# Cross-attention and FFN on one core: probabilities turned in 32x32 blocks by VectorE in the middle groups, and weighted sums in sixteen tiles of the array

## The chip, the cores and the metric

The kernel runs on one core of one Trainium2 chip. The metric is the time of one execution in microseconds of the device. Before the change three runs gave 793.26, 792.1 and 794.7 us, with a median of 793.26 us. All arithmetic on the path spoken of here is float32.

## The reference, cut to what matters

There are 16 batches of 128 rows and 1024 columns, with 32 query heads of 32 columns; four query heads share one of 8 key and value heads.

```
Q = layernorm(x) @ Wq + bq;  K = ctx @ Wk + bk;  V = ctx @ Wv + bv
w = softmax(Q K^T / sqrt(32))            # per batch and head, 128 x 128
x = x + (w @ V) @ Wo + bo
x = x + scale * (ei(layernorm(x)) @ kernel)   # ei: last 20% of the columns times -4
```

What the change concerns is `w @ V`: for each batch and head, probabilities of 128 queries by 128 keys times values of 128 keys by 32 columns. TensorE contracts over partitions, so the keys must lie on the partitions of both operands; the exponentials leave ScalarE with the queries on the partitions.

## The kernel before, in words

The 16 batches go in eight groups of two (`GB = 2`). A group has four **attention steps**, one for each batch `b` and half `a` of the heads (16 query heads each): the steps `q = 0..3` of line 970 have b0 a0, b1 a0, b0 a1, b1 a1. Beside these steps TensorE has **dense work**: the output projection of the group before (`out_proj`, matmuls on line 661), keys and values of the next group (`prep_k`, `prep_v`, line 322), queries of the next group (`prep_q`, line 450) and the FFN (`ffn`, line 322).

The order of all instructions is written by a planner in the kernel, the class `Stream`. Dense work is a queue of generators; each piece yields its estimated length, which advances a planned clock. `later(us, fn)` puts a small piece of other work (a normalization, a division, a transpose) at a planned time; `run(until)` emits pieces and what has come due. The planned lengths set the order in which instructions stand on each engine and nothing else: the engines then wait for one another only through data.

One attention step is `attend` (line 754) and `weighted` (line 605). `scores` (line 560) issues 16 matmuls of 32 contraction rows, four for each of four PSUM tiles (`ps_sc`, four buffers of one bank); a tile `i` holds four heads (`NG = 4`) that share a key head. For each tile VectorE finds the negated maximum (line 579), ScalarE does four exponentials with their row sums (line 583), VectorE takes the reciprocal (line 594) and multiplies (line 595). Then `turn` has TensorE transpose the four 128x128 blocks (line 600) into PSUM and ScalarE copies the result to SBUF (line 602). At the step's end `weighted` does four matmuls of 128 keys by 32 columns, with 512 moving columns each (line 610), into one PSUM bank, the four in four column strips of the array, and ScalarE copies the bank (line 618). The next step's scores follow at once.

On TensorE each float32 matmul that is not a transpose stands in the program as two pairs of a weight load and a matmul with the same operands (5024 pairs on the page); these are called **passes** here. A transpose is one pass.

The first group (group 0) and the last (group 7) have loops of their own; groups 1 to 6 are the **middle groups**, 24 attention steps. All loads and stores go through SP's queue in the planned order; the weights of the projections come as pieces of 512 KB into a ring of eight buffers (`fetch`, line 219). The normalized rows of the FFN of early groups go through DRAM (`through_dram`, line 301), and VectorE then turns and splits them (`split_blocks`, line 719), at the planned delays `FBACK` (line 822).

## Time and profile before

| | |
|---|---|
| median of three runs | 793.26 us |
| the profiled execution: its own time / its span | 793.75 / 792.0 us |
| granted TensorE clock, mean | 0.997 |
| busy: TensorE / VectorE / ScalarE | 770.7 / 484.9 / 322.7 us |
| DMA | 190.31 MB, mean 240 GB/s |
| one matmul record of line 610 (512 columns) | 619 ns mean, 256 records |
| one matmul record of line 567 (128 columns) | 283 ns mean, 1024 records |
| VectorE, one 32x32-block transpose of 128x512 float32 (lines 348, 370, 727) | 699 to 703 ns |
| VectorE, the multiplication on line 595 | 716 ns mean, 128 of them |
| ScalarE, copy of 128x512 from PSUM (lines 602, 618) | 591 and 585 ns |
| ScalarE, activation of 128x128 (lines 583, 437) | 369 and 368 ns |

Records of matmuls overlap, since the array is pipelined: a mean length is not what one of them costs. What it costs is the distance to the next one's start, which the chain of waits and the timeline give. The rows of one engine in the timeline are merged where they follow one another; "idle before" stands in brackets with what ended it.

### The profile page before, as it was taken

What the parts mean: (1) busy time and instruction counts of PE and PEld (TensorE: products, weight loads), DVE (VectorE), ACT (ScalarE), POOL (GpSimd) and SP (SyncE); (2) the same over time, 40 slices, a digit from 0 to 9 for tenths busy, and PEclk for the clock granted to TensorE, in tenths of its full rate; (3) what the DMA queues carried; (4) which work ended last, traced back from release to release, by engine and by line L of the source; (5) the groups of instructions that cost most, each with busy time, mean ns of one, the idle gap of its engine ahead of it and who ended that gap; (6) DMA issues with size and microseconds to landing.
All of it is one profiled execution on the core that took longest, in us unless ns stands there. A gap on an engine that the chain in (4) does not pass through costs nothing.

```text
span 792.0 us, 13741 instructions
## 1 busy us (share of the span) xinstructions
PE 770.7 (97%) x5024; PEld 572.8 (72%) x5024; DVE 484.9 (61%) x882; ACT 322.7 (41%) x1261; POOL 107.3 (14%) x133
## 2 busy tenths in 40 slices
PE   5998999999999999999999999999999999999997
PEld 4886794589746996479855898568974799546566
DVE  1258647756766667466774667755676756667442
ACT  0254764434344443344533444343434445466100
POOL 1153703020010102020020200102001100100300
PEclk9999999999999999999999999999999999999999
DMA  9999799979698776978688786977769567562502
GB/s 211 361 299 296 251 382 390 267 209 305 221 310 232 239 239 214 314 210 264 219 264 263 196 287 212 302 233 209 260 217 321 190 204 243 184 195 81 205 34 80
DMA packets 98483, 190.31 MB, mean 240 GB/s; under 512 B 8016, under 2 KB 57168, under 8 KB 98416
## 3 DMA queue, kind: packets, MB, share of 16 engines
q1 hardware_dynamic: 96544, 187.73, 73.5%
q10 hardware_dynamic: 1728, 1.57, 1.0%
q8 instruction: 40, 0.66, 0.3%
q14 instruction: 27, 0.22, 0.1%
q0 software_dynamic: 144, 0.14, 0.1%
HBM read 160.04 MB, written 29.36 MB: 239 GB/s over the span
## 4 chain that ended last, share of the span: by engine, by line
PE 89%; DMA 4%; DVE 2%; issue 2%; POOL 1%; ACT 0%; SPq 0%; POOLq 0%
PE f L322 15%; PE o_u L661 13%; PE q_u L450 13%; PE o_v L661 7%; PE tpp L600 7%; PE q_v L450 6%; PE v L322 5%; PE k L322 5%; PE sc L567 4%; PE av L610 4%; PE q L322 3%; PE q_c L450 3%; PE o_c L661 3%; DMA piece<-o 1%; DMA wv_sb<-in_L_xattn_Wv_dram 1%
## 5 line engine op out<-in xcount | busy, mean ns | idle before, releaser
L583 ACT ACTIVATE p<-sc,negm 128x128 f32<-128x128 f32 x512 | 181.4, 369 | 140.0 <-DVE negm L579 75.9
L602 ACT COPY pt<-tpp 128x512 f32<-128x512 f32 x128 | 74.5, 591 | 143.8 <-PE tpp L600 143.4
L579 DVE TENSOR_REDUCE negm<-sc 128x4 f32<-128x512 f32 x128 | 86.7, 680 | 53.8 <-PE sc L567 53.7
L322 PE MATMUL f<-wf_sb,x2l 128*128 128x512 f32 x256 | 105.4, 412 | 0.0
L583 ACT ACTIVATION_READ_ACCUMULATOR p<-sc,negm 128x1 f32 x512 | 105.3, 206 | 0.0
L322 PE MATMUL f<-wf_sb,x2h 128*128 128x512 f32 x256 | 101.1, 395 | 0.0
L595 DVE TENSOR_TENSOR p<-p,inv 128x512 f32<-128x512 f32 x128 | 91.6, 716 | 4.4
L450 PE MATMUL q_u<-t,piece 128*128 128x128 f32 x672 | 80.9, 275 | 0.0
L600 PEld LDWEIGHTS tpp<-ident,p 128*128 128x128 f32 x512 | 62.0, 141 | 25.5 <-issue 17.0
L600 PE MATMUL tpp<-ident,p 128*128 128x128 f32 x512 | 75.9, 273 | 4.5 <-DVE p L595 3.1
L450 PEld LDWEIGHTS q_u<-t,piece 128*128 128x128 f32 x672 | 77.9, 192 | 0.0
L184 POOL TENSOR_TENSOR x<-x,bo_b 128x256 f32<-128x256 f32 x64 | 54.1, 871 | 154.2 <-DMA x<-in_x_dram 94.0
L322 PE MATMUL v<-wv_sb,cT 128*128 128x256 f32 x256 | 61.9, 391 | 9.4 <-DMA wv_sb<-in_L_xattn_Wv_dram 9.2
L661 PE MATMUL o_v<-piece,s 128*128 128x512 f32 x128 | 60.4, 598 | 0.5 <-DVE x L675 0.5
L322 PEld LDWEIGHTS v<-wv_sb,cT 128*128 128x128 f32 x256 | 48.3, 196 | 15.8 <-issue 9.2
L661 PE MATMUL o_u<-piece,s 128*128 128x512 f32 x128 | 59.1, 594 | 0.6 <-DVE x L675 0.6
L322 PE MATMUL k<-cT,wk_sb 128*128 128x256 f32 x256 | 58.1, 380 | 1.2 <-DVE cT L348 1.2
L661 PE MATMUL o_u<-piece,yT 128*128 128x512 f32 x128 | 58.5, 599 | 0.0
L322 PEld LDWEIGHTS f<-wf_sb,x2l 128*128 128x128 f32 x256 | 48.2, 188 | 11.0 <-issue 1.1
L322 PEld LDWEIGHTS f<-wf_sb,x2h 128*128 128x128 f32 x256 | 48.2, 188 | 10.2 <-issue 0.5
L322 PEld LDWEIGHTS k<-cT,wk_sb 128*128 128x128 f32 x256 | 47.9, 190 | 10.5 <-issue 2.6
L567 PEld LDWEIGHTS sc<-kT,qT 32*128 32x128 f32 x1024 | 31.5, 186 | 26.5 <-issue 26.5
(83 smaller groups left out, 932.5 us busy)
## 6 DMA issues: line engine op xcount, KB each, us to landing
piece<-o SPq DMA_DIRECT2D x64, 512.0 KB, 4.7
piece<-q SPq DMA_DIRECT2D x56, 512.0 KB, 5.1
piece<-in_L_xattn_Wq_dram SPq DMA_DIRECT2D x50, 512.0 KB, 5.3
piece<-in_L_xattn_Wo_dram SPq DMA_DIRECT2D x48, 512.0 KB, 4.6
xn<-in_x_dram SPq DMA_DIRECT2D x16, 512.0 KB, 6.7
x<-in_x_dram SPq DMA_DIRECT2D x16, 512.0 KB, 4.8
ctx<-in_ctx_dram SPq DMA_DIRECT2D x60, 128.0 KB, 6.6
out_dram<-x SPq DMA_DIRECT2D x15, 512.0 KB, 2.7
```

The lines of the kernel that those rows point to most:

```text
L184: lambda cut=cut: nc.gpsimd.tensor_add(x_t[:, cut], x_t[:, cut], bo_b[:, cut]) and None,
L322: nc.tensor.matmul(mm, lhsT=lhsT, rhs=rhs, start=k == 0, stop=k == n - 1)
L450: nc.tensor.matmul(mm if part is None else mm[:, part], lhsT=lhsT, rhs=rhs, start=start and n == k == 0, stop=k == len(some) - 1, skip_gro ...
L567: nc.tensor.matmul(tiles[i][:, g], lhsT=qT[rows, g], rhs=kT[rows, a, cols], start=True, stop=True,)
L579: nc.vector.tensor_reduce(negm, tile_, AX.X, ALU.max, negate=True)
L583: nc.scalar.activation(p[:, g], tile_[:, g], AF.Exp, bias=negm[:, g : g + 1], accum_out=total[:, g : g + 1],)
L595: nc.vector.tensor_mul(p, p, inv.unsqueeze(2).to_broadcast([P, NG, S]))
L600: nc.tensor.transpose(tp[:, g], p[:, g], ident)
L602: nc.scalar.copy(pt, tp)
L610: nc.tensor.matmul(mm[i * HD : (i + 1) * HD], lhsT=vs[b][:, h * HD : (h + 1) * HD], rhs=pts[i], start=True, stop=True,)
L661: nc.tensor.matmul(mm, lhsT=lhsT[:, 2 * k + c], rhs=w[:, c], start=start and k == c == 0, stop=k == c == 1, skip_group_check=True,)
```

## The change

In the middle groups alone:

- **Turning.** The TensorE transposes and the ScalarE copies of `turn` go. VectorE transposes each tile of probabilities in place, in 32x32 blocks (`turn_blocks`). Block (k, t) of a head then has key `32 t + r` on partition `32 k + r` and the queries of block k along the row.
- **Scaling.** For tiles 0 and 1 of a step VectorE makes the reciprocal only and ScalarE multiplies, in four activations with a scale by row (`scale_rows`). Tiles 2 and 3 are scaled on VectorE as before.
- **Weighted sums.** `weighted_blocks` has 64 matmuls of 32 keys by 32 columns with 128 moving columns, 16 for each `t`, one on each of the 16 tiles of 32x32 of the array; the four `t` accumulate. The result lies in four PSUM banks (a bank for each row strip `k`), from which one ScalarE copy gathers `yT`.
- **PSUM.** The pool `ps_sc` holds one tile of four banks instead of four of one; the scores and the weighted sums of the middle groups take turns in it. Scores have one tile of four banks in all groups.
- **Values.** Since each row strip needs the values of all keys on its own 32 partitions, `prep_v` stores the values of a middle batch to DRAM (128 KB), and `load_values` reads them back four times (four DMAs of 128 KB) into one half of `pt_all`, a constant tile in place of the four buffers `pt`. The first and last groups use `pt_all` for turned probabilities as `pt` was used.
- **Order.** The planned length of a middle step goes from 23.2 to 21.5 (in group 6 from 21.0 to 19.6). `weighted_blocks` stands 4.0 planned us ahead of the step's end, and dense work follows it before the next scores: 1.72 us in the steps q = 0, 1.7 to 3.3 us in the others, by the durations that the same pieces have in the trace of before. `FBACK` goes from 22 and 24 to 16 and 18, so that the rows of the FFN are turned and split sooner.

```diff
-    ps_sc = ctx.enter_context(tc.tile_pool(name="ps_sc", bufs=4, space=PSUM))
+    ps_sc = ctx.enter_context(tc.tile_pool(name="ps_sc", bufs=1, space=PSUM))
...
             vs[b] = v
+            if GB <= b < B - GB:
+                stream.later(2.0, lambda b=b, v=v: nc.sync.dma_start(out=v_dram[b], in_=v) and None)
...
-        tiles = [ps_sc.tile([P, NG, S], FP, tag="sc", name=f"sc_{b}_{a}_{i}") for i in range(NI)]
+        sc = ps_sc.tile([P, NI, NG, S], FP, tag="sc", name=f"sc_{b}_{a}")
...
+    def scale_rows(p, inv):
+        for g in range(NG):
+            nc.scalar.activation(p[:, g], p[:, g], AF.Copy, scale=inv[:, g : g + 1])
+
+    NK = S // HD
+    pt_all = const.tile([P, NI, NG * S], FP, name="pt_all")
...
+    def repeated(b):
+        vr = pt_all[:, 2 * (b % GB) : 2 * (b % GB) + 2].rearrange("p i n -> p (i n)")
+        return vr.rearrange("p (t n) -> p t n", t=NK)
+
+    def load_values(b):
+        for k in range(NK):
+            nc.sync.dma_start(
+                out=repeated(b)[k * HD : (k + 1) * HD],
+                in_=v_dram[b].rearrange("(t r) n -> r t n", t=NK),
+            )
+
+    def turn_blocks(p):
+        blocks = p.rearrange("p g (t k) -> p g t k", t=NK)
+        nc.vector.transpose(blocks, blocks)
+
+    def weighted_blocks(b, a, pts):
+        av = ps_sc.tile([P, NK, NG, S], FP, tag="sc", name=f"av_{b}_{a}")
+        for t in range(NK):
+            for i in range(NI):
+                head = slice(i * HD, (i + 1) * HD)
+                for k in range(NK):
+                    rows = slice(k * HD, (k + 1) * HD)
+                    nc.tensor.matmul(
+                        av[head, k, :, :HD],
+                        lhsT=repeated(b)[rows, t, a * P + i * HD : a * P + (i + 1) * HD],
+                        rhs=pts[i][rows, :, t * HD : (t + 1) * HD],
+                        start=t == 0,
+                        stop=t == NK - 1,
+                    )
+        yTs[b, a] = work.tile(S4, FP, tag="yT", name=f"yT{b}_{a}", bufs=4)
+        nc.scalar.copy(yTs[b, a].rearrange("p g (k q) -> p k g q", k=NK), av[:, :, :, :HD])
...
+                def by_vector():
+                    divide(b, a, i, p, total)
+                    turned()
+                def by_both():
+                    inv = inverse(b, a, i, total)
+                    stream.later(1.6, lambda: scale_rows(p, inv))
+                    stream.later(3.6, turned)
+                def turned():
+                    turn_blocks(p)
+                    pts[i] = p
...
+                if length is None:
+                    stream.later(2.3, by_both if i < 2 else by_vector)
...
-    FBACK = ((7.0, 22.0), (8.0, 24.0))
+    FBACK = ((7.0, 16.0), (8.0, 18.0))
...
-            length = 17.4 if first else 23.2 if grp < NGRP - 2 else 21.0
+            length = 17.4 if first else 21.5 if grp < NGRP - 2 else 19.6
...
+                    pts = attend(b, a)
+                    stream.run(start + length - 4.0)
+                    stream.run(stream.now, lambda: None in pts)
+                    weighted_blocks(b, a, pts)
+                    stream.now += 2.1
...
+                        stream.run(start + length)
+                if q == 2 * NA - 1 and first:
+                    load_values(nxt * GB)
+                if q >= 2 * NA - (1 if first else 2) and nxt < NGRP - 1:
+                    load_values(nxt * GB + q % GB)
```

More of the change, by code (lines that the diff above doesn't have):

```diff
@@ L567, in scores @@
                 nc.tensor.matmul(
-                    tiles[i][:, g],
-                    lhsT=qT[rows, g],
-                    rhs=kT[rows, a, cols],
-                    start=True,
-                    stop=True,
+                    sc[:, i, g], lhsT=qT[rows, g], rhs=kT[rows, a, cols], start=True, stop=True
                 )
-        return tiles
+        return sc
     def exponentials(b, a, i, tile_):
@@ L590, in exponentials, with inverse, divide @@
         return p, total
-    def divide(b, a, i, p, total):
+    def inverse(b, a, i, total):
         inv = small.tile([P, NG], FP, tag="inv", name=f"inv_{b}_{a}_{i}")
         nc.vector.reciprocal(inv, total)
+        return inv
+    def divide(b, a, i, p, total):
+        inv = inverse(b, a, i, total)
         nc.vector.tensor_mul(p, p, inv.unsqueeze(2).to_broadcast([P, NG, S]))
+    def scale_rows(p, inv):
[3 more added lines that the diff above has]
+    pt_all = const.tile([P, NI, NG * S], FP, name="pt_all")
+    v_dram = [dram.tile([P, KV], FP, name=f"v_dram{b}") for b in range(B)]
     def turn(b, a, i, p):
@@ L600, in turn @@
             nc.tensor.transpose(tp[:, g], p[:, g], ident)
-        pt = work.tile([P, NG, S], FP, tag="pt", name=f"pt_{b}_{a}_{i}", bufs=4)
-        nc.scalar.copy(pt, tp)
-        return pt
+        nc.scalar.copy(pt_all[:, i].rearrange("p (g s) -> p g s", g=NG), tp)
+        return True
     def weighted(b, a, pts):
@@ L612, in weighted @@
                 lhsT=vs[b][:, h * HD : (h + 1) * HD],
-                rhs=pts[i],
+                rhs=pt_all[:, i],
                 start=True,
@@ L618, in weighted @@
         nc.scalar.copy(yTs[b, a], mm)
+    def repeated(b):
[25 more added lines that the diff above has]
+        yTs[b, a] = work.tile(S4, FP, tag="yT", name=f"yT{b}_{a}", bufs=4)
+        nc.scalar.copy(
+            yTs[b, a].rearrange("p g (k q) -> p k g q", k=NK), av[:, :, :, :HD]
+        )
     x2Ts, x2ns, x2stats = {}, {}, {}
@@ L752, in ffn, with attend @@
             nc.sync.dma_start(out=out[b], in_=x_t)
-    def attend(b, a, length):
-        tiles = scores(b, a)
+    def attend(b, a, length=None):
+        sc = scores(b, a)
         stream.now += 1.2
@@ L762, in first, with by_tensor @@
             def first(i=i):
-                p, total = exponentials(b, a, i, tiles[i])
-                stream.later(2.3, lambda: divide(b, a, i, p, total))
-                def third():
+                p, total = exponentials(b, a, i, sc[:, i])
+                def by_vector():
+                    divide(b, a, i, p, total)
+                    turned()
+                def by_both():
+                    inv = inverse(b, a, i, total)
+                    stream.later(1.6, lambda: scale_rows(p, inv))
[3 more added lines that the diff above has]
+                    pts[i] = p
+                def by_tensor():
                     pts[i] = turn(b, a, i, p)
                     return 0.45
-                stream.later(length / 2 - 3.0, third)
+                if length is None:
+                    stream.later(2.3, by_both if i < 2 else by_vector)
+                else:
+                    stream.later(2.3, lambda: divide(b, a, i, p, total))
+                    stream.later(length / 2 - 3.0, by_tensor)
             stream.later(0.7 + 2.4 * i, first)
@@ L972 @@
                 start = stream.now
-                pts = attend(b, a, length)
-                if q == 2 * NA - 1:
-                    stream.run(start + length - 2.0, lambda: stream.queue)
-                else:
-                    stream.run(start + length - 2.0)
-                stream.run(stream.now, lambda: None in pts)
-                weighted(b, a, pts)
-                stream.now += 1.0
+                if first:
+                    pts = attend(b, a, length)
+                    if q == 2 * NA - 1:
+                        stream.run(start + length - 2.0, lambda: stream.queue)
+                    else:
+                        stream.run(start + length - 2.0)
+                    stream.run(stream.now, lambda: None in pts)
+                    weighted(b, a, pts)
+                    stream.now += 1.0
+                else:
+                    pts = attend(b, a)
+                    stream.run(start + length - 4.0)
+                    stream.run(stream.now, lambda: None in pts)
+                    weighted_blocks(b, a, pts)
+                    stream.now += 2.1
+                    if q == 2 * NA - 1:
+                        stream.run(start + length, lambda: stream.queue)
+                    else:
+                        stream.run(start + length)
[3 more added lines that the diff above has]
+                    load_values(nxt * GB + q % GB)
         stream.add(
```

## The prediction

> **What bounds the kernel now.** I read the page's first part, then the busy time by stretch for one whole middle group, then the chain of waits inside that group. The stretch from 430.96 to 524.96 us is one period: the same product of the output projection starts at both ends, and the periods before it have the same length.

> ```profile
> PE 770.7 (97%) x5024; PEld 572.8 (72%) x5024; DVE 484.9 (61%) x882; ACT 322.7 (41%) x1261; POOL 107.3 (14%) x133
> ```

> ```profile
> core 0: us, PE busy (x) PEld busy (x) DVE busy (x) ACT busy (x) POOL busy (x), PEclk, DMA share, GB/s
> ...
> 430.96:524.96 94.00, 94.00 (x634) 70.72 (x633) 61.19 (x112) 38.62 (x156) 9.10 (x12) 1.00 0.78 247
> ```

> TensorE is busy through the whole 94.00 us at full clock; VectorE has 33 us to spare and ScalarE 55. So a middle group lasts as long as TensorE's own work, and what TensorE no longer does shortens it, until another engine's result comes late. The chain, in order of time, shows what the removed work costs:

> ```profile
> 444.77 0.44 PE tpp L600 x4
> 445.21 1.73 PE v L322 x8
> 446.94 0.44 PE tpp L600 x4
> 447.37 2.59 PE v L322 x12
> 449.96 1.00 PE av L610 x8
> 450.96 1.10 PE sc L567 x32
> 452.06 3.77 PE q_u L450 x32
> ```

> Only TensorE appears. Four transposes take 0.44 us, the weighted sums of a step (8 passes) 1.00 us, the scores (32 passes) 1.10 us.

> **Removed from TensorE.** Shares of this chain over the period: transposes 7.4%, weighted sums 4.2%, together 11.6% of 94.0 = 10.9 us, or 2.73 us for each of four steps (4 x 0.435 + 0.995). In 24 steps that is 65.5 us.

> **Added to TensorE: the one large unknown.** A step gets 64 matmuls, which as float32 are 128 passes of 128 moving columns. The trace has no matmul of 32x32, so I bound it by the two tiled ones, here as the timeline of the weight loads has them.

> ```profile
> 426.88 0.16 PEld L610 LDWEIGHTS av<-pt,v 128*32 128x32 f32 x8 [0.76 <-issue]
> 426.88 1.07 PE L610 MATMUL av<-pt,v 128*32 128x512 f32 x8
> ...
> 427.87 0.98 PEld L567 LDWEIGHTS sc<-kT,qT 32*128 32x128 f32 x32 [0.84 <-issue]
> 427.87 1.17 PE L567 MATMUL sc<-kT,qT 32*128 32x128 f32 x32
> ```

> All eight weight loads of the weighted sums fall within 0.16 us, though the matmuls last 1.07. In the single records four matmuls start 7 ns apart on four strips, and the next four one pass later: 112 ns later for the scores' 128 columns, about 0.45 us for 512. Different strips thus run beside one another. The scores' 32 passes on four strips are eight waves of 112 ns = 0.90 us, and 1.10 in the chain, so entering and leaving costs 0.2.

> - Low end: all sixteen tiles run at once, as four do now. 128 / 16 = 8 waves x 112 ns = 0.9, plus 0.2 = **1.1 us**.
> - High end: no more than the four at once that the trace shows. 128 / 4 = 32 waves x 112 ns = 3.6, plus 0.2 = **3.8 us**.
> - Between them: the rate at which TensorE's sequencer hands out instructions. A dense matmul gives it 111 ns or more for a pair, so that it is never seen as a limit now, but a 16-tile burst of 256 instructions in 1.1 us would ask for 4 ns each. The nearest records are two semaphore waits of TensorE with eight loads and matmuls between them, at 49.862 and 49.987 us: the queue was empty there. The same distance of 0.125 us stands at 138.671. A wait itself takes 51 ns, which leaves 74 ns for eight instructions, 9.25 ns each or 18.5 ns a pass. At waits inside dense stretches the sequencer is 17 pairs ahead of the array, so 17 of the 128 are already queued. The other 111 x 18.5 ns = 2.05 us, and I add 0.05 for the entry that this does not cover: **2.1 us**.

> I take 2.1: it rests on records of this sequencer, and the low end needs a rate twice as high as any that the trace shows with an empty queue. Per step 2.73 - 2.1 = 0.63 us is saved, in 24 steps **15.1 us**. With the ends: 39 us saved at 1.1, 26 us lost at 3.8.

> [...]

> **VectorE.** Per period 16 block transposes are added at 0.70 us (the 128x512 float32 rows of lines 348, 370 and 727 are 699 to 703 ns), and 8 multiplications at 0.716 go: +11.2 - 5.7 = +5.5 us, so 66.7 of some 91.5 us. The reciprocals stay. This hides under TensorE as long as the last tile of a step is turned before its weighted sums come. Now the last multiplication of a middle step ends 11.5 to 12.8 us after the scores. Four transposes (+2.8), two multiplications less (-1.4), and, in the third step of a group, 2.1 us of the FFN rows' turning and splitting that `FBACK` moves ahead of it, put it at 13 to 16.5 us. The dense work between scores and sums, by the durations in the trace, is 17.2 to 18.0 us in groups 1 to 5, 14.6 to 15.4 in group 6. Covered by 1 to 4 us in the former, by nearly nothing in the latter: I add **1 us** in all, for waits in group 6. Without the cover each us late costs 24 us; the bounds are 0 and 1.5 us a step, the second if ScalarE's and VectorE's turns fall badly.

> **ScalarE.** Per period 16 copies of 591 ns go (9.5 us) and 32 scalings of 128x128 come (nearest row: 368 ns on line 437; 11.8 us). It stays near 41 of 91 us: nothing. The scaling stands between two exponentials, and the transposes of tiles 0 and 1 wait for it on VectorE; queued behind them are the last tile's reciprocal and multiplication. That is part of the 1 to 4 us above.

> **A new wait: scores behind the gather.** Scores and weighted sums now share four banks, so the next scores wait until ScalarE has copied `yT`. The copy starts 0.1 us after the sums now and takes 0.585; say 0.8 us with the signal back. Dense work of 1.7 us or more stands between. Cost nothing; if ScalarE were held up by 2 us there, 1 us a step would show. Queued behind waiting scores is all of TensorE. The nearest case of a longer copy is the strided read of four banks; the block-transposed splits on line 728 (620 ns against 591 plain) say that strides cost little.

> **SP and DMA.** Per period 2 stores and 8 loads of 128 KB are added, 1.25 MB on 23 MB. The DMA share is 0.78, so 0.84 at the shorter period. Loads of 128 KB land in 6.6 us (context rows), and the first use is a step's 17 us or more after the issue. The loads wait in SP's queue for the last sums that read the old half, and the weight pieces stand behind them, in a ring of eight. Nothing, with bounds of 0 and 5 us, once, where group 0 ends with all eight loads together. PSUM for the scores in the last group: the four banks were needed together before as well; nothing.

> **Sum.** 793.75 (the profiled execution, 792.0 of span) - 15.1 + 1 = 779.6; the median of the runs lies 0.5 us under the profiled one, so **779 us**.

> **The rivals.**
> - *Sixteen tiles at once, no sequencer limit*: 1.1 to 1.4 us a step. 793 - 24 x 1.33 to 1.63 + 1 = 755 to 762. For it: strips run beside one another now without loss in both directions. Against it: 4 ns an instruction. Chance 0.15.
> - *Slower: the tiled burst is held to few tiles or to a slow hand-out*. The mechanism is the rate of passes in `weighted_blocks`, nothing else; it decides from 2.73 us a step, 21 ns a pass. [...] For it: no more than four in flight are seen. Against it: 18.5 ns from the semaphore records is an upper bound of the hand-out. Chance 0.18.
> - *VectorE takes the bound*: 2.1 us a step as forecast, but the last tile turns up 0.5 to 1 us late in each of 24 steps: 779 + 12 to 24 = 791 to 803, about no change. For it: third steps and group 6 are tight. Against it: VectorE busy 73%. Chance 0.12.
> - *The forecast*, 1.8 to 2.4 us a step and up to 3 us of waits: 771 to 788. Chance 0.55.

> **The numbers.** The range reaches from the first rival to the lower part of the second: 755 to 804 leaves out about 0.03 below and 0.15 above. What this kernel's measurement can tell from no change is about 0.3%, 2.4 us. Faster by more: 0.15 + 0.55 + a little of the third = 0.72. Within: 0.08 of the third. Slower: 0.18 and a rest of the third = 0.20.

> **What would show it.** In the chain of the changed kernel's middle period: no `tpp`, the weighted sums near 2.1 us a step, the scores still 1.10, a period near 91.5 us. Sums at 1.1 or above 2.7 us show the rivals. Waits of the sums for VectorE's transposes beyond 0.1 us a step, outside group 6, show the third; waits of the scores for the `yT` copy, or of the sums for DMA, would show a cost that I put at nothing.

## The result, and the profile after

Four runs of the changed kernel gave 797.5 to 808.3 us, with a median of 800.11; the kernel before gave a median of 793.23 beside them. The ratio is 1.0106, with a 95% interval of 1.008 to 1.0133: **slower by about 1%**, where 779 us were forecast. The runs also scatter more: 10.8 us between the fastest and the slowest, against 2.6 before. The profiled execution took 797.8 us, with a span of 796.0, 4.0 us more than before. The granted clock is 0.997 in both.

The page's first part of the changed kernel, and two middle groups in the busy time by stretch, each from the first scores of the group to the first scores of the next:

```profile
PE 759.6 (95%) x7520; PEld 567.5 (71%) x7520; DVE 512.3 (64%) x930; ACT 322.8 (41%) x1357; POOL 107.6 (14%) x133
```

```profile
core 0: us, PE busy (x) PEld busy (x) DVE busy (x) ACT busy (x) POOL busy (x), PEclk, DMA share, GB/s
338.11:430.57 92.46, 91.76 (x1049) 69.49 (x1048) 65.54 (x120) 38.45 (x170) 9.10 (x12) 1.00 0.85 264
430.57:523.89 93.32, 92.14 (x1049) 69.86 (x1049) 65.72 (x120) 38.45 (x170) 9.10 (x12) 1.00 0.86 263
```

TensorE has 11 us less to do than before, as meant, but is no longer busy all the time: before, the 93.99 us of a period were 93.99 us of work; here 0.7 to 1.2 us of each are idle, and groups differ where they were alike. The chain of waits inside such a group (the dependent work, followed back in time) shows that the planned trade took place:

```profile
351.54 5.18 PE v L322 x24
356.72 1.83 PE av L661 x102
358.55 1.92 PE v L322 x8
360.48 1.10 PE sc L569 x32
```

No `tpp` is left, the scores take 1.10 us as before, and the weighted sums take **1.83 us**, less than the 2.1 of the forecast: 14.3 ns for each of 128 passes (the chain leaves out some records that overlap, so that its count reads 102; the page has all 3072 of the 24 steps). Dense work is entered once more, since the scores no longer follow the sums at once: the eight `v` matmuls between the two take 1.92 us where eight take 1.73 elsewhere. So an undisturbed step gains 2.73 - 1.83 - 0.19 = 0.71 us. The distances between scores agree: the first steps of groups 2 to 5 go from 22.93 to 22.22 us, where nothing disturbs them, and the second steps from 23.02 to 22.30. In 24 steps that would be 17 us. It is lost again in many small places. TensorE's waits:

```profile
...
PE q_u L452 <- DVE qT L554: 3.4, 5, 1.2
PE o_u L714 <- DVE x L728: 2.7, 1, 2.7
PE sc L569 <- issue: 1.9, 2, 1.4
PE av L661 <- issue: 1.8, 2, 1.2
PE q_v L452 <- issue: 1.4, 1, 1.4
...
PE o_v L714 <- issue: 1.0, 1, 1.0
```

The columns are the sum in us, the number and the longest of such waits; the two larger rows above them belong to the start of the program and to group 0. Two things stand out. None of these waits is that of the middle groups' sums for VectorE's turned tiles, which the forecast held to be the danger. And four rows have "issue" as what ended the wait: TensorE waited for nothing that the profile shows. The kernel before has no such row.

By groups, from the first scores of each to those of the next (group 7: to the last matmul), in us of the profiled executions. The columns e6, e14 and e15 are experiments told below:

| | before | after | e6 | e14 | e15 |
|---|---|---|---|---|---|
| group 0 | 79.38 | 81.63 | 79.13 | 79.12 | 79.51 |
| group 1 | 95.64 | 99.39 | 101.22 | 100.55 | 96.12 |
| group 2 | 93.99 | 92.60 | 91.62 | 93.07 | 91.62 |
| group 3 | 93.99 | 93.11 | 92.99 | 92.99 | 92.83 |
| group 4 | 93.99 | 93.43 | 93.89 | 94.35 | 92.17 |
| group 5 | 93.99 | 94.60 | 93.38 | 94.23 | 92.05 |
| group 6 | 86.71 | 85.80 | 86.00 | 88.41 | 85.62 |
| group 7 | 107.75 | 109.08 | 107.74 | 107.76 | 108.05 |

Groups 0 and 7 have the arithmetic of before and yet lose 2.25 and 1.33 us; group 1 loses 3.75; groups 2 to 6 should win 2.8 each and win between 1.4 and less than nothing.

### The profile page after: what moved, and what is told of

It is laid out like the page before. It is cut to its first block, busy times and chain, and to the rows that moved or that the text cites. A ratio compares the mean times of both kernels' runs of the same rounds, so it can differ in the third digit from the quotient of the medians.

```text
span 796.0 us, 18805 instructions
## 1 busy us (share of the span) xinstructions
PE 759.6 (95%) x7520; PEld 567.5 (71%) x7520; DVE 512.3 (64%) x930; ACT 322.8 (41%) x1357; POOL 107.6 (14%) x133
## 4 chain that ended last, share of the span: by engine, by line
PE 69%; DVE 14%; ACT 5%; issue 4%; DMA 4%; POOL 1%; SPq 1%; ACTq 0%; DVEq 0%; POOLq 0%
PE o_u L714 12%; PE f L322 8%; PE q_u L452 7%; PE o_v L714 6%; PE v L322 6%; PE av L661 5%; PE k L322 5%; PE sc L569 4%; PE q_v L452 4%; ACT p L581 3%; PE q L322 3%; PE o_c L714 3%; DVE p L650 2%; DVE negm L577 2%; DVE p L597 2%
## 5 line engine op out<-in xcount | busy, mean ns | idle before, releaser
L322 PE MATMUL f<-wf_sb,x2l 128*128 128x512 f32 x256 | 104.7, 409 | 0.8 <-DVE x L798 0.6
L322 PE MATMUL f<-wf_sb,x2h 128*128 128x512 f32 x256 | 101.2, 395 | 0.0
L669 ACT COPY yT<-av 128x512 f32<-128x512 f32 x24 | 14.1, 586 | 138.6 <-PE av L661 138.6
L322 PE MATMUL v<-wv_sb,cT 128*128 128x256 f32 x256 | 61.6, 394 | 9.0 <-DMA wv_sb<-in_L_xattn_Wv_dram 9.0
L650 DVE STREAM_TRANSPOSE p<-p 128x512 f32<-128x512 f32 x96 | 66.5, 701 | 2.0 <-ACT p L602 0.4
L322 PEld LDWEIGHTS v<-wv_sb,cT 128*128 128x128 f32 x256 | 49.4, 197 | 16.9 <-issue 10.1
L602 ACT ACTIVATE p<-p,inv 128x128 f32<-128x128 f32 x192 | 60.9, 405 | 0.0
L597 DVE TENSOR_TENSOR p<-p,inv 128x512 f32<-128x512 f32 x80 | 57.9, 723 | 2.8
L322 PEld LDWEIGHTS f<-wf_sb,x2l 128*128 128x128 f32 x256 | 48.1, 188 | 15.6 <-DVE x L798 3.0
L322 PE MATMUL k<-cT,wk_sb 128*128 128x256 f32 x256 | 56.9, 380 | 1.2 <-DVE cT L348 1.2
L322 PEld LDWEIGHTS k<-cT,wk_sb 128*128 128x128 f32 x256 | 48.5, 190 | 10.8 <-issue 2.9
L322 PEld LDWEIGHTS f<-wf_sb,x2h 128*128 128x128 f32 x256 | 48.2, 188 | 10.7 <-issue 0.5
L661 PE MATMUL av<-p,pt_all 32*32 32x128 f32 x3072 | 46.4, 278 | 1.8 <-issue 1.8
```

The source lines that it names most:

```text
L322: nc.tensor.matmul(mm, lhsT=lhsT, rhs=rhs, start=k == 0, stop=k == n - 1)
L597: nc.vector.tensor_mul(p, p, inv.unsqueeze(2).to_broadcast([P, NG, S]))
L602: nc.scalar.activation(p[:, g], p[:, g], AF.Copy, scale=inv[:, g : g + 1])
L650: nc.vector.transpose(blocks, blocks)
L661: nc.tensor.matmul(av[head, k, :, :HD], lhsT=repeated(b)[rows, t, a * P + i * HD : a * P + (i + 1) * HD], rhs=pts[i][rows, :, t * HD : (t ...
L669: nc.scalar.copy(yTs[b, a].rearrange("p g (k q) -> p k g q", k=NK), av[:, :, :, :HD])
```

## The experiments

Four theories came out of this comparison. **W**: one PSUM tile of four banks makes engines wait that did not wait when there were four tiles. **C**: TensorE's program reaches it in blocks, and a burst of 256 short instructions uses a block up before the next is there. **D**: VectorE's order (the FFN rows sooner, more work for each tile) delays what TensorE waits for. **T**: the stores and loads of the values cost time, through SP's queue or as traffic. Times are medians of the runs of one kernel; ratios are to the kernel before on the same chip.

### e1, e2: the PSUM tile

The waits of the changed kernel have a row that the kernel before does not have:

```profile
DVE negm L577 <- ACT p L581: 35.5, 39, 2.4
```

The maximum of a tile on VectorE waits 39 times for the exponentials of the tile before it on ScalarE, though the two lie in different banks. e1 takes the changed kernel and gives it four tiles again, for the scores and for the sums (`yT` is then copied in four instructions of 0.27 us in place of one of 0.59); e2 takes the kernel before and does nothing but make the four tiles one.

```diff
# e1, to the changed kernel
-    sc = ps_sc.tile([P, NI, NG, S], FP, tag="sc", name=f"sc_{b}_{a}")
+    sc = [ps_sc.tile([P, NG, S], FP, tag="sc", name=f"sc_{b}_{a}_{i}") for i in range(NI)]
# e2, to the kernel before
-    tiles = [ps_sc.tile([P, NG, S], FP, tag="sc", name=f"sc_{b}_{a}_{i}") for i in range(NI)]
+    sc = ps_sc.tile([P, NI, NG, S], FP, tag="sc", name=f"sc_{b}_{a}")
+    tiles = [sc[:, i] for i in range(NI)]
```

> The changed kernel, but the four banks are four tiles again (scores one tile for each i, weighted sums one tile for each k, four ScalarE copies of 128x128 for yT). Theory W (one tile for four banks makes each maximum on VectorE wait for the exponentials of the tile before it, 35.5 us of new waits in the profile): these waits vanish, third steps of a group get back some 0.8 us and fourth steps 0.4, groups 0 and 7 some 3 us: about 790 us. Theory C (code fetch of TensorE stalls it for 6 us): its stalls stay; alone it gives no gain, 797 to 800. Theory D (the FFN rows that are turned sooner crowd VectorE): at most 2 us of gain, 796 to 798.

> The kernel before, with the scores in one tile of four banks, nothing else. Theory W: the waits of VectorE's maxima for ScalarE come, some 20 to 40 us of them; middle groups have 4 us of cover a step and lose little, groups 0 and 7 lose 2 to 4 us: 795 to 797 us. Theories C and D: no change, 793 us.

e2 took 797.25 us, a ratio of 1.0055 (1.0038 to 1.0072): **this one edit alone makes the old kernel 4 us slower.** Its waits have the new row, and those of TensorE that have grown or are new:

```profile
DVE negm L580 <- ACT p L584: 22.1, 28, 2.4
...
PE tpp L601 <- DVE p L596: 4.2, 2, 3.2
...
PE sc L568 <- ACT p L584: 1.2, 2, 0.9
PE av L611 <- ACT pt L603: 1.2, 1, 1.2
```

In the kernel before, the first of these three is 3.1 us and the other two are not there.

Its middle groups are unchanged to 0.01 us (93.99) but for group 6, and groups 0 and 7 take 81.61 and 109.05, as in the changed kernel. In the middle groups TensorE covers the wait; in two steps of group 0 (25.46 and 20.51 us for 24.40 and 19.33), and in group 7, where steps follow each other every 12 to 13 us, it does not. In e1 the row is gone and groups 0 and 7 take 79.15 and 107.75 again, so the 3.6 us are this. The median only went to 798.24, ratio 1.0068 (1.0043 to 1.0093), and not to 790: group 1 took 101.23 there, and the third steps, which W should have mended as well, still take 23.34 us. W holds and is not the whole.

### e3: instructions in blocks

The idle times "<-issue" stand in the middle of bursts, with all operands there. The timeline of TensorE in the changed kernel:

```profile
148.35 1.17 PE L569 MATMUL sc<-kT,qT 32*128 32x128 f32 x31
150.93 0.37 PE L569 MATMUL sc<-kT,qT 32*128 32x128 f32 x1 [1.42 <-issue]
```

Thirty-one of the 32 passes of the scores have run, and the last starts 1.42 us late. The page's list of DMA queues has the clue:

```profile
q8 instruction: 59, 0.97, 0.5%
```

TensorE's program, as built, has grown from 10,251 instructions in 656,064 B to 15,201 in 972,864 B, 64 B each; this queue moves 59 packets of 16,384 B, so 256 such instructions in a packet (15,201 / 59 = 258). Before, it moved 40 (10,251 / 40 = 256):

```profile
q8 instruction: 40, 0.66, 0.3%
```

Laid against the program, all six stalls of this kind in the groups 1 to 6 are at an instruction whose number is 196 or 197 modulo 256. In the trace's packet records a fetch takes 1.1 us in the mean, 0.9 to 1.4 us. At the six stalls the last fetch starts 1.2 to 3.4 us after TensorE entered the block that it then runs out of, and TensorE goes on 2.3 to 2.7 us after the fetch's start: 3.7 to 6.1 us in all. The kernel before needs at least 11.8 us for a block; the changed one passes some in 2.7 us.

e3 puts 48 transposes of a constant (96 instructions) at the front of the program, which shifts all later block ends against the work.

```diff
+    pad = ps_tp.tile([P, 4, P], FP, tag="tp", name="pad")
+    for n in range(48):
+        nc.tensor.transpose(pad[:, n % 4], ident, ident)
```

> The changed kernel with 48 more TensorE transposes of the identity at the very start, where TensorE waits for its first loads; they shift all later TensorE instructions by 96 places. Theory C: stalls without a data releaser stand again at places with the remainder 197 after division by 256 in the program, so at other matmuls than in the changed kernel (six there); 2 to 8 us in all, time 795 to 803. Rival (these stalls are data or semaphore waits of those matmuls): they stand at the same matmuls as in the changed kernel, their remainders moved by 96.

802.35 us, 1.0116 (1.008 to 1.0152). The stalls were at other matmuls, and again all at 196 or 197 modulo 256. The longest came after 89 passes of a burst of sums that the changed kernel passes undisturbed:

```profile
620.90 0.85 PE L664 MATMUL av<-p,pt_all 32*32 32x128 f32 x39 [2.81 <-issue]
```

The stall goes with the place in the program and not with the data. C holds as to the place; what it costs, e9 and e11 show better. In one point it is incomplete: before this stall TensorE had been in the block for 20.1 us, 16 of them dense work, and the fetch started only 17.5 us after its entry; the other two long stalls of e3 (1.11 and 2.03 us) came after blocks of 11.6 and 9.0 us, and e4, e6, e13 and e14 have one such stall each (0.7 to 2.3 us, after 13 to 15 us). In all of them TensorE goes on 2.4 to 2.6 us after the fetch's start. So a fetch can come late in a block that is not short as well; why it does stays open.

### e4, e5, e6: rows at their old place, no values

```diff
# e4, to the changed kernel
-    FBACK = ((7.0, 16.0), (8.0, 18.0))
+    FBACK = ((7.0, 22.0), (8.0, 24.0))
```

> The changed kernel with FBACK at 22 and 24 as before. Theory D: third steps lose their waits for VectorE, 0.8 us in each of five groups: 793 to 795 us. Theory W: these waits come from the maxima that wait for ScalarE; little changes, 796 to 800 us.

796.6 us, 1.0051 (1.0033 to 1.0068). The third step of an undisturbed middle group goes from 23.34 to 22.53 us. TensorE's timeline in the changed kernel at that place, and then the same product in e4, where it follows without a wait:

```profile
280.77 2.17 PE L452 MATMUL q_v<-t,piece 128*128 128x128 f32 x18
283.49 3.39 PE L452 MATMUL q_u<-t,piece 128*128 128x128 f32 x28 [0.54 <-DVE qT L554]
```

```profile
284.73 2.51 PE L452 MATMUL q_u<-t,piece 128*128 128x128 f32 x21
```

The addition `qT` on VectorE, which frees the PSUM tile for the next product, stands behind a turned FFN row, a sum for the queries and a turned tile. Five such steps at 0.8 us: 4 us for D. The median is above the 793 to 795 that D was to give, with 8.5 us of stalls at block ends in its profile.

e5 leaves the stores and loads of the rearranged values out of the changed kernel, so that the weighted sums of the middle groups use what happens to lie there:

```diff
-            if GB <= b < B - GB:
-                stream.later(2.0, lambda b=b, v=v: nc.sync.dma_start(out=v_dram[b], in_=v) and None)
...
-                if q == 2 * NA - 1 and first:
-                    load_values(nxt * GB)
-                if q >= 2 * NA - (1 if first else 2) and nxt < NGRP - 1:
-                    load_values(nxt * GB + q % GB)
```

> The changed kernel without the stores of the values and without their loads; the weighted sums of the middle groups read what lies in the constant tile, so this part of the result is left out. Theory V (eight loads at the end of group 0 hold SP's queue for 10 us, and the rows of x behind them come late to VectorE): the 2.7 us wait of the output projection in the first step of group 1 goes and groups 0 and 1 get 3 to 5 us back: 793 to 797 us. Theory C: with 8 MB less traffic the code fetches may come sooner, but stalls at the remainder 197 remain, over 2 us in all. If V is wrong: 798 to 801 us.

792.89 us, 1.0003 (0.9983 to 1.0023): the values cost about 7 us, and what is left is level with before. The wait of 2.7 us in group 1's first step, which was expected to go, stays. By groups, the profile gets back 2.4 us in group 0, 1.9 in group 1 and 3.0 in groups 2 to 6. Group 0 takes 79.19 us here, though the PSUM tile is one: in this execution W's loss there did not show, and why is open. e6 has e1 and e4 together.

> Four tiles in place of one, and FBACK at 22 and 24 as before, together. If theories W and D each describe a loss of its own (W: 3 to 4 us, in groups 0 and 7; D: 0.8 us in each third step of groups 2 to 6 and some in the fourth): about 792 to 795 us, with the losses of group 1 and the code fetches left. If both are the same loss: 796 to 798 us.

794.19 us (790.4 to 800.0), 1.0019 (0.9992 to 1.0046). Without W and D, with C and T, the changed kernel is level with the kernel before within this interval. Group 2 takes 91.62 us, which is the period of 91.5 that was forecast; group 1 takes 101.22.

### e7, e8: other ways for the values

At the end of group 0 eight loads of values go through SP's queue together and hold it for 9.92 us, and the rows of `x` and weight pieces stand behind them:

```profile
122.49 9.92 SPq L643 DMA_DIRECT2D pt_all<-v_dram  x8
132.57 0.96 SPq L173 DMA_DIRECT2D xn<-in_x_dram  x2
```

e7 issues all loads of values from GpSimd's queue; e8 puts the odd batch's four behind the first step of group 1. Both start from e6.

```diff
# e7
-            nc.sync.dma_start(
+            nc.gpsimd.dma_start(
                 out=repeated(b)[k * HD : (k + 1) * HD],
# e8
-                if q >= 2 * NA - (1 if first else 2) and nxt < NGRP - 1:
+                if grp == 1 and q == 0:
+                    load_values(b0 + 1)
+                if not first and q >= 2 * NA - 2 and nxt < NGRP - 1:
                     load_values(nxt * GB + q % GB)
```

> As the run with four tiles and the late FBACK, but the loads of the values are issued from GpSimd's queue, so that nothing stands behind them on SP. Theory V: the loss of 4 us in the first step of group 1 goes, 787 to 792 us. Rival (the traffic itself is late, whatever queue issues it): no gain over the run with SP's queue; GpSimd's own work (rs, on which VectorE waits) may come late and lose 1 to 4 us.

> As the run with four tiles and the late FBACK, but at the end of group 0 only the values of the even batch are loaded, those of the odd batch after the first step of group 1 (one step before their use). Theory V: half of the hold on SP's queue remains, so half of the loss in the first step of group 1 (some 2 us) comes back: 790 to 793 us. Rival (the traffic, not the queue): no change against the run with all eight loads.

793.86 us, 1.0012 (0.9992 to 1.0032), and 795.9 us, 1.0024 (1.0002 to 1.0046): both like e6, so by the medians neither moves anything, and the 787 to 792 and 790 to 793 of theory V were missed. In the profiles TensorE's wait in group 1's first step is 2.75 and 2.73 us, still for VectorE's addition to `x`. The runs of each lie 8 us apart, from 790.4 to 799.5 in both together, which is more than the effect that was looked for.

### e9, e11: shorter bursts

e9 starts from e8 and emits the 128 passes in two bursts of 64, with dense work planned at 3 us between them (1.5 in group 6). e11 starts from e8 and leaves out half of the sums: two of the four blocks of keys.

```diff
# e9
+                    gap = 3.0 if length > 20.0 else 1.5
-                    stream.run(start + length - 4.0)
+                    stream.run(start + length - 4.0 - gap)
                     stream.run(stream.now, lambda: None in pts)
-                    weighted_blocks(b, a, pts)
-                    stream.now += 2.1
+                    weighted_blocks(b, a, pts, 0)
+                    stream.now += 1.05
+                    stream.run(start + length - 2.95)
+                    weighted_blocks(b, a, pts, 1)
+                    stream.now += 1.05
# e11
-        for t in range(NK):
+        for t in range(2):
```

> The changed kernel with four separate PSUM tiles, the FFN rows at their old place, the odd batch's values loaded one step later, and the 128 passes of a step's weighted sums in two bursts of 64, with about 3 us of dense work between them (1.5 us in group 6). Theory C (TensorE's program arrives in blocks of 256 instructions, and a burst that runs through a block in less than about 4 us waits for the next): the stalls of 0.3 to 2.8 us inside bursts go or shrink below 1 us in all; one more entry into the small tiles costs about 0.2 us in each of 24 steps, and the runs scatter less: 788 to 793 us against about 795 with one burst. Rival (the stalls are the end of a semaphore wait or of PSUM, not of instruction supply): stalls of the same number and size, 796 to 800. If the first burst now comes before VectorE's last block transposes, waits for it show in the third and fourth steps, up to 1 us each, and eat the gain.

> Leaves out half of the computation of the weighted sums in the middle groups (only two of the four blocks of keys), so its output is not the reference's; the rest as in the run with separate tiles, rows at their old place and values loaded in two parts. A burst is then 64 passes, 128 instructions. Passes at 14.3 ns each: 0.92 us a step less, 22 us in 24 steps. Theory C: the stalls inside bursts go too, 3 to 6 us more, 767 to 771 us in all with little scatter. Rival (stalls not from instruction supply): 772 to 775 with stalls as before.

The distances between the first and the next other matmul give the lengths of the bursts. All 24 bursts of scores in groups 1 to 6 together take 26.48 us in the kernel before, 29.94 in the changed one, and again **26.48 in e9 and in e11**. The shortest passage of a block is 5.0 us in e9 and 6.1 in e11. e11 has no stall at a block's end at all, e9 one of 0.39 us, and e9's four runs lie within 1.4 us. This settles C for the bursts: those of 128 instructions hardly outrun the supply here, and those of 256 with the scores soon behind them do. In the changed kernel this costs 3.5 us in the scores, 2.6 in the sums and 2.4 in dense matmuls at a block's end right behind a burst: 8.5 us in the profiled run, of which 6.2 are idle time and the rest passes that follow one another slowly. It can be only part of what differs from run to run: the four runs of e11, whose profile has no such stall, still lie 6.3 us apart.

The cure did not pay. e9 took 797.59 us, 1.0049 (1.0034 to 1.0064). Its chain:

```profile
258.42 1.73 PE v L322 x8
260.14 1.00 PE av L665 x51
261.14 3.65 PE v L322 x16
264.80 1.00 PE av L665 x56
```

Two bursts cost 2.00 us in place of 1.83, and the 16 `v` after the first take 3.65 in place of 3.45: some 0.36 us a step, which halves the gain (a second step takes 22.65 us). And the first burst comes before VectorE is done:

```profile
PE av L665 <- DVE p L650: 6.3, 8, 1.2
PE av L665 <- DVE inv L592: 3.0, 1, 3.0
```

Nine waits of 9.3 us in all: this is the rival of VectorE's bound, called up by the earlier place. e11 took 773.11 us, 0.9723 (0.9685 to 0.976): an undisturbed second step takes 21.46 us, 0.84 less than with all passes, 20 us in 24 steps, and the stalls are gone besides. The time lies in the rival's range (772 to 775) and not in C's (767 to 771), though the stalls, in which the two differ, are gone; five waits for weight pieces, 5.1 us in all, have come up.

### e10: all four tiles scaled by ScalarE

```diff
# to e8
-                    stream.later(2.3, by_both if i < 2 else by_vector)
+                    stream.later(2.3, by_both)
```

> As the run with separate tiles, rows at their old place and values loaded in two parts, but ScalarE scales all four tiles of a middle step, so that VectorE has two multiplications of 0.7 us less in each step. Theory: the fourth steps, and the first step of group 1, wait for VectorE (additions to x behind the tiles' turning); they gain 0.3 us in each of five groups and some 2 us once: 791 to 793 us. Rival: VectorE has slack nearly everywhere and ScalarE's two more scalings make the last tile later: no change or up to 3 us slower, 794 to 799.

797.59 us, 1.0053 (1.0025 to 1.0082); the theory's 791 to 793 was missed. The fourth steps did gain, in undisturbed groups 24.14 and 24.21 us for 24.58 in e8; group 1's first step did not. ScalarE is now late with the copy of the sums, and the scores wait for it, which the changed kernel does not show:

```profile
PE sc L569 <- ACT yT L671: 2.3, 6, 0.8
```

### e12: no values, and the burst in halves

From e6 with the values left out as in e5 and the burst split as in e9.

> Leaves out the stores and loads of the rearranged values (so the output is not the reference's), and has separate PSUM tiles, the FFN rows at their old place and the burst in two halves. If the losses are what the runs so far show (one PSUM tile 3.5 us, rows 4, instruction supply about 6, values 7 less what they share), the time is 793 - 17 for the gain + 5 for the second entry into the small tiles + 2 to 4 for the first step of group 1 = 782 to 786 us. If it stays above 790, a cause of some 6 us or more is still unnamed.

796.54 us, 1.0038 (1.0023 to 1.0053): above the 782 to 786 that was expected. The split brings a loss of its own: group 1's first step takes 30.32 us with a wait of 3.0 for VectorE, and the steps are those of e9. So e12 does not close the account; e15 tries to. But against e9, which has the values, it is only 1 us faster, within the intervals, where e5 was 7 us faster than the changed kernel: with short bursts the values cost next to nothing. That fits a cost that comes through the supply of instructions; that VectorE's waits hide it here is not excluded.

### e13, e14, e15: what group 1 waits for, and the limit

In the first step of group 1 TensorE stands for 2.73 us between two products of the output projection. The timelines of TensorE and VectorE in the changed kernel:

```profile
134.65 3.60 PE L714 MATMUL o_v<-piece,s 128*128 128x512 f32 x8
140.97 3.70 PE L714 MATMUL o_u<-piece,s 128*128 128x512 f32 x8 [2.73 <-DVE x L728]
```

```profile
137.14 1.27 DVE L282 BATCH_NORM_STATS2 st_a<-xn 128x6 f32<-128x512 f32 x2
...
139.51 0.81 DVE L291 TENSOR_SCALAR xq<-xn,mv_a,rs_a 128x1024 f32<-128x1024 f32 x1 [0.66 <-POOL rs_a L290]
140.23 0.68 DVE L728 TENSOR_TENSOR x<-o_u,x 128x512 f32<-128x512 f32 x1
```

The addition to `x` that frees the PSUM tile stands on VectorE behind the statistics of the queries' rows and a visit to GpSimd. Before, it stood there as well, but 16 transposes of probabilities, 1.74 us, lay between TensorE's products of this step, and the waits were 0.6 and 0.5 us: the removed work was a cover. e13 starts from e6 and plans the statistics 3 us later in this group; e14 also moves the odd batch's loads behind those of `x`; e15 is e13 without the values, as in e5.

```diff
# e13
-                stream.later((10.0 if grp == 2 else 5.0) + 4.0 * j, lambda b=b: rows_x(b))
+                stream.later((13.0 if grp == 2 else 5.0) + 4.0 * j, lambda b=b: rows_x(b))
# e14, to e13
+                if grp == 1 and q == 0:
+                    stream.later(8.0, lambda b1=b1: load_values(b1))
...
-                if q >= 2 * NA - (1 if first else 2) and nxt < NGRP - 1:
+                if not first and q >= 2 * NA - 2 and nxt < NGRP - 1:
                     load_values(nxt * GB + q % GB)
```

> The changed kernel with separate PSUM tiles and the FFN rows at their old place (794.2 us), and in group 1 the statistics of the queries' rows 3 us later in the plan, so that VectorE does the addition to x that TensorE's next product waits for ahead of them. Theory V (the transposes on TensorE had covered this wait; VectorE's order causes it): the gap of 4.2 us before the fourth product of the output projection goes, or falls below 1 us: 790 to 791.5 us, ratio about 0.996. Rival (the gap comes from SP, held 10 us by the values' loads, so that the rows come late and a later wait takes its place): the gap moves to a later place in group 1, 793.5 to 795 us.

> As the run before with the odd batch's four loads of values behind the loads of x on SP. Theory: with VectorE's order mended the loads cost nothing, so the same as the run before within 1 us. Rival (SP's hold delays x and the residuals): 1 to 3 us faster than the run before.

> Leaves out the stores and loads of the rearranged values, so that its output is not the reference's; separate PSUM tiles, the FFN rows at their old place and the statistics later. If the known losses are all, what is left is the gain of about 17 us less the stalls of instruction supply (4 to 6 us), the third and last steps that wait for VectorE (group 6, 3 us): 783 to 787 us. If the traffic of the values costs nothing in itself, 788 to 791, as with it.

In e13 the addition comes in time (133.78 us), and the gap stays, with another releaser; in e14 it is gone. TensorE's timeline of e13, then of e14:

```profile
131.29 3.60 PE L714 MATMUL o_v<-piece,s 128*128 128x512 f32 x8
137.72 3.67 PE L714 MATMUL o_u<-piece,s 128*128 128x512 f32 x8 [2.83 <-DMA piece<-o]
```

```profile
132.24 3.60 PE L714 MATMUL o_v<-piece,s 128*128 128x512 f32 x8
135.67 3.60 PE L714 MATMUL o_u<-piece,s 128*128 128x512 f32 x8
```

So both theories were right: two waits end at nearly the same place, VectorE's and that for a weight piece behind the values in SP's queue, and taking one away shows the other (e8, with half of the loads moved and VectorE's order left, had 2.73 us for VectorE). With both gone the step takes 23.07 us in place of 25.21. Yet the medians are 798.75, 1.0056 (1.0035 to 1.0076), and 798.36, 1.0068 (1.0047 to 1.009), no better than e6: in the profiled runs the stalls at block ends came to 8.4 and 10.1 us, against 5.8 in e6 (those over 0.2 us), and used the gain up.

e15 took **783.76 us, 0.9864 (0.9843 to 0.9884)**, as expected. Its group 2:

```profile
217.24:308.86 91.62, 91.37 (x1049) 69.44 (x1048) 65.19 (x120) 39.28 (x182) 9.06 (x12) 1.00 0.80 253
```

With the same matmuls in the same order as e13, the bursts of scores take 27.04 us in place of 31.35, and the idle time at block ends is 3.3 us in place of 8.4. e5 shows the same against the changed kernel, 3.6 us for 6.2. The DMA share of a middle group is 0.80, against 0.85 and 0.86 in the changed kernel. That the values' traffic delays the fetches is argued from these numbers and from e12; it was not tried by itself (for instance with loads that nobody uses), and the profiles are of one execution each. Of the 14.4 us between the profiled executions of e13 and e15, 5.1 are this idle time, 5.4 three waits for weight pieces, of which e15 has none, and 1.7 waits for VectorE's additions in the FFN; the rest, some 2 us, stays open. No run with the whole computation beat the kernel before.

## Why the prediction was wrong

The trade itself, fewer microseconds of TensorE's own work, came out a little better than forecast. What failed is the step from there to the time: the sum holds 1 us for everything that TensorE would wait for, and it waited for its program, for VectorE and ScalarE, and for loads, some 20 us in all.

- **The weighted sums** ("the one large unknown"): size nearly right, 1.83 us for 2.1. The term of 18.5 ns a pass was too high; 128 passes on sixteen tiles went at 14.3 ns. Whether the hand-out of instructions sets this rate, as the forecast had it, no run shows. The upper end of the range, 804 us, holds 11 us for sums of 3.2 us a step; no run shows that term: the sums took 1.83 us, and 2.00 us in two bursts (e9).
- **The saving of 0.63 us a step** became 0.71, although the 0.19 us of a second entry into dense work were not in the sum. 17 us were won in place of 15.1, where nothing disturbed. The period of 91.5 us was met in group 2 of e6 and e15, at 91.62.
- **"PSUM for the scores in the last group: the four banks were needed together before as well; nothing"**: failed. It asked whether there is room, not who waits for whom. One tile of four banks made VectorE wait for ScalarE 39 times, and cost 3.6 us in groups 0 and 7 (e1 and e2 show it both ways; in e5's profile group 0 is without it).
- **The supply of instructions**: failed, and for the sign it weighs most. The forecast asked how fast the sequencer hands out instructions that it has; it did not ask whether it has them. The number was on the page: 40 packets of 16 KB. It cost 8.5 us, and by the small scatter of e9 it has a part in that of the runs.
- **"This hides under TensorE"**, with 1 us added for group 6: the sums did not wait, as forecast, but the forecast looked only at the turned tiles. Other things on VectorE were late: `qT` in the third steps (4 us, e4), the addition to `x` in group 1's first step (1.3 us net), the FFN's additions in the fourth steps, which gain 0.3 us and not 0.7 (2 us; TensorE's waits for them show 0.6 of it, and e10, with less work on VectorE, gets 0.4 a step back).
- **SP and DMA: "Nothing, with bounds of 0 and 5 us, once, where group 0 ends with all eight loads together"**: the place was right (e13). But as a whole the values cost far more: 7 us (e5 against the changed kernel) to 15 us (e15 against e13), about a third of it in stalls at block ends.
- **The scores behind the gather**: nothing, as forecast; the wait appeared only when ScalarE got two scalings more (e10).

The losses named, 8.5 + 3.6 + 4 + 1.3 + 2, and 0.5 that group 6 lost besides, are 20 us; with 17 us of gain and the 4 us that the profiled run lost they should be 21, so that some 1 us is not assigned. What the values cost is not added to these, since e5 gets it back in part in the same places (group 0, block ends). Of the rivals none took place as described; "slower" came from causes that were on no list of rivals.

## What to carry to other kernels

Count instructions as well as time: here TensorE stood for its program in the middle of bursts, for up to 1.4 us in the changed kernel and 2.8 us in e3. In the changed kernel it took 3.7 to 6.1 us from entering a block of 256 instructions to going on behind its end, where that end stalled; in the kernel before, a block took 11.8 us or more. How many instructions a new burst has can be counted before the change. Since a fetch came late in some long blocks too (9.0 to 20.1 us in e3), blocks longer than this do not exclude stalls. When work leaves the bound engine, look at each place where it stood for what it covered: here two waits of 2.73 and 2.83 us ended at nearly the same place (the changed kernel and e13), and removing one showed the next. The change of how the PSUM buffer is cut into tiles was a change of who waits for whom (39 waits of VectorE for ScalarE, 35.5 us), and the groups that it did not mean to touch paid for it, 3.6 us.
